# A GPS layer on one core: marks in POOL's gather queue, a rearranged first part, a look-up accumulated in PSUM, and packing operands read from PSUM

## The chip, the core and the metric

The kernel runs on one core of one Trainium2 chip. The core has a matrix engine (PE, whose weight loads the profile lists as PEld), a vector engine (DVE), an activation engine (ACT), a general engine (POOL) and a queue engine (SP), each with an instruction stream of its own that is executed in order; they meet through semaphores. The metric is the device time of one launch in microseconds (us), the median of several runs. The profile is one further execution, taken by the hardware profiler.

## What is computed

One layer over 6250 nodes of 256 features with 206,250 edges (200,000 and one self loop per node), all in fp32. The three parts, cut to what matters:

```python
xn = layernorm(x)
# 1. graph attention, 4 heads of 64 features
h = xn @ W;  el = h @ Wl.T;  er = h @ Wr.T
e = exp(leaky_relu(el[src] + er[dst], 0.2))
w = e / segment_sum(e, src)[src]
gnn = elu(stack([segment_sum(w[:, k:k+1] * h[dst], src) for k in range(4)]) + b)
# 2. linear attention, 4 heads of 32, with 4 memory keys and values
q, k, v = split(xn @ w_qkv)            # softmax of q over features, of k over nodes
mix = rmsnorm(context(softmax(k), v) . softmax(q) @ w_out) + xn
x = x + gnn + mix
# 3. mixture of 8 experts, top 2, hidden width 256
t = layernorm(x)
x = x + t + sum_e combine[:, e] * (gelu(t @ w1[e]) @ w2[e])
```

The edges come sorted by dst, and the sums run over src.

## The kernel before

The nodes are cut into 49 tiles of 128 rows (NT), the edges into 1612 columns of 128.

**First part.** `project` takes groups of four tiles. It computes the layernorm statistics, the normalised rows xn (DVE, L310), their transposes (PE, L316), and one product pr with all the projection weights (L321). From pr, ACT copies q, k and v (L325) and a row of a table, which holds the 64 features of h and its er values (L328). DVE copies el (L329) and keeps a running maximum kmax of k (L335). SP stores four tiles of the table to memory. Between the groups run the 51 calls of `sort_batch`, which sort the edges of 32 columns (BW) by source tile pair: a one-hot ob of the bin, counts n_ps per column by PE (L371), their running sum on DVE (L375) and, by subtraction, the counts before each column (L380), ranks by two matmuls (L398, L399: `tri` is a strictly upper triangular matrix), which ACT casts to r16 (L404), DVE multiplies by ob (L410) and sums over the 26 bins (L413). L415 writes each rank twice, side by side, since the 16-bit DVE operations of this kernel work on pairs. A permutation matmul then lays the edges of each bin together in `grid` (L433). Last, `context` computes exp(k − max) (L468, L469) and the context of the linear attention, interleaved with the remaining sort batches.

**Main part.** It runs over the 25 pairs of node tiles. `pack(q)` brings the edges of one pair into 36 columns per tile (CW; 35 of them, CPT, hold edges). For 101 blocks of edges, 16 at a time, DVE builds the one-hots ohc (L858) and ohp (L870) by comparing positions with an iota, and rc (L865, twice) as the product of ohc and the packed values of grid; PE multiplies them into s_ps (L875). From s_ps come the table rows to fetch, dst_x (L884, L886), and the rows within the tile, loc (L894). `gather` then issues 35 indirect DMAs per tile on POOL (L906), 1715 in all, each of which fetches 128 table rows into a column of an xe tile. An xe tile has seven columns, a node tile needs five of them, and the pool has eight. `pack(q + 1)` is called while the first tile of pair q is summed.

`look(b, k)` fetches el for each edge: a one-hot oh of loc (DVE, L919), its transposes (PE, L932, and ACT, L936), a product with three bf16 summands of el (e_ps, L939), and a reduction over the three (er, L943). The edges of a tile lie in four quarters (S) of rows; a quarter's columns begin at multiples of eight (CS) and reach 12 columns (GC), so that neighbours overlap. `weights` adds the overlapping er together (L960, L961, L963, L964), adds the gathered er part of xe (L967, five times), and applies leaky ReLU and exp; the result ew_s is written to a PSUM tile named bank (L972). `sums(k)` multiplies oh by ew_s (ohw, L980) and PE accumulates 45 products with xe into a_ps (L987). The xe tiles are free when their last product is done.

Between these steps a generator puts in the attention outputs and the expert products of earlier blocks of four tiles (h_ps L731, y_ps L747, x L751, store L759). A tile scheduler turns dependencies into semaphore waits and keeps each engine's order as it lays it out. On POOL a gather waits for loc or dst_x only where it is the first of its pack, for the freeing of an xe tile at the first of seven columns, and, always, for the landing of the gather eight back.

**Tail.** After the last tile follow the remaining expert steps and a branch for overfull tiles, which these data do not take.

Of the kernel before, what the change touches and what calls it, by code (L numbers as in the profile page):

```python
# [17 lines left out]
P = 128  # L18
GT = 4
# [6 lines left out]
EB = 7  # L26
S = 4
# [8 lines left out]
def tile_gps_layer(  # L36
# [174 lines left out]
    tri = sp.tile([P, P], F16, name="tri")  # L211
    nc.vector.tensor_scalar(tri, iota_f, piota, None, op0=OP.is_gt)
# [3 lines left out]
    starts = sp.tile([NB, BW // CB, CB], F32, name="starts")  # L216
    nc.vector.memset(starts, 1.0)
    nc.vector.memset(starts[:, :, 0:1], 0.0)
# [69 lines left out]
    def project(t0, n):  # L288
# [16 lines left out]
        tab = qw.tile([P, GT, TW], F32, name="tab")  # L305
        nc.gpsimd.memset(tab[:, :, TW - 1:TW], 1.0)  # L306
        for j in range(n):
            t = t0 + j
            xn = qw.tile([P, D], F32, name="xn")
            nc.vector.tensor_scalar(  # L310
                xn, xt[:, j, :], stats[:, t, 0:1], rstd[:, t:t + 1],
                op0=OP.subtract, op1=OP.mult,
# [15 lines left out]
            nc.scalar.copy(tab[:, j, :TW - 1], pr[:, O_TAB:O_EL])  # L328
            nc.vector.tensor_copy(el[:, t, :], pr[:, O_EL:PW])  # L329
            rows = P if t < NT - 1 else last  # L330
            k_t = kv[:rows, t, :HID]
            if t == 0:
                nc.vector.tensor_copy(kmax, k_t)
            else:
                nc.vector.tensor_max(kmax[:rows], kmax[:rows], k_t)  # L335
        nc.sync.dma_start(
            out=table[t0 * P:(t0 + n) * P, :].rearrange("(t p) f -> p t f", p=P),
            in_=tab[:, :n, :],
# [9 lines left out]
    def sort_batch(t):  # L348
# [20 lines left out]
        n_ps = sps.tile([NB, BW], F32, name="n_ps")  # L369
        for c in range(w):  # L370
            nc.tensor.matmul(  # L371
                n_ps[:, c:c + 1], lhsT=ob[:, c, :], rhs=ones16[:, 0:1], start=True, stop=True
            )
        inc = sw.tile([NB, BW], F32, name="inc")
        nc.vector.tensor_tensor_scan(  # L375
            inc[:, :w], flat(starts)[:, :w], n_ps[:, :w], 0.0,
            op0=OP.mult, op1=OP.add,
        )
        before = sw.tile([NB, BW, 2], F16, name="before")
        nc.vector.tensor_tensor(  # L380
            before[:, :w], inc[:, :w, None].to_broadcast([NB, w, 2]),
            n_ps[:, :w, None].to_broadcast([NB, w, 2]), op=OP.subtract,
        )
        if w == BW:
            nc.scalar.copy(ntot[:, bs], inc[:NQ].rearrange("q (b c) -> q b c", c=CB)[:, :, CB - 1])
        else:
            for b, e in enumerate(ends):
                nc.scalar.copy(ntot[:, bs][:, b:b + 1], inc[:NQ, e - 1:e])
        ahead = sw.tile([NB, BW, NB], F16, name="ahead", bufs=1)
        nc.vector.tensor_tensor(  # L390
            pairs(ahead[:, :w]), two(before[:, :w], NB // 2), row(delta, NB // 2), op=OP.mult
# [3 lines left out]
        for i, a in enumerate(range(0, w, BB)):  # L395
            z = min(w, a + BB)
            part = r_ps[:, i, :(z - a) * NB]
            nc.tensor.matmul(part, lhsT=tri, rhs=flat(ob[:, a:z]), start=True, stop=False)  # L398
# [12 lines left out]
        rank = sw.tile([P, BW], F16, name="rank")  # L411
        with nc.allow_low_precision("one summand of each sum is not zero"):
            nc.vector.tensor_reduce(rank[:, :w], r16[:, :w], axis=AX.X, op=OP.add)  # L413
        rank2 = sw.tile([P, BW, 2], F16, name="rank2")
        nc.vector.tensor_copy(rank2[:, :w], rank[:, :w, None].to_broadcast([P, w, 2]))  # L415
# [25 lines left out]
    def context():  # L441
        km_ps = mps.tile([HID, P], F32, name="tp")
# [23 lines left out]
        for t0, n in groups:  # L466
            kk = kv[:, t0:t0 + n, :HID]
            nc.vector.tensor_sub(kk, kk, krow[:, None, :].to_broadcast([P, n, HID]))  # L468
# [333 lines left out]
    yps = gx.enter_context(tc.tile_pool(name="yp", bufs=2, space=PSUM))  # L802

# [3 lines left out]
    gb_s = bank[:, 512 - FO:]  # L807
# [7 lines left out]
    def pack(q):  # L815
# [8 lines left out]
        for u in range(U):  # L824
# [6 lines left out]
            total = pe.tile([P, S, NBT], F32, name="e_ps")  # L831
# [21 lines left out]
        iota_2 = pairs(iota_h)[:, None]  # L853
        s_ps = pl.tile([P, 2, U * CW], F32, name="s_ps")
        for t0 in range(0, NBT, PB):
# [8 lines left out]
            for i in range(2):  # L864
                nc.vector.tensor_tensor(  # L865
                    pairs(rc[:, :m, i, :]), pairs(ohc[:, :m]),
                    twos(grid[:, q, t0:t0 + m, i, :], U * CW // 2), op=OP.mult,
# [31 lines left out]

# [15 lines left out]
    def look(b, k):  # L915
# [10 lines left out]
        elif k < 3:  # L926
# [19 lines left out]
            )  # L946

    def weights(xes, er):
        z = gw.tile([P, CW, H], F32, name="z")

        def of(q0, n, a, m):

# [225 lines left out]
```

## Time and profile before

| | us |
|---|---|
| median of 3 runs | 3158.25 |
| lowest, highest run | 3149.09, 3170.76 |
| profiled execution | 3989.86 |
| its span | 3988.1 |
| first gather begins | 491.6 |
| gathers, one | 0.944, in steps of 1.25 |
| idle of POOL ahead of gathers | 1901.0 |

The profiled execution took 831.6 us longer than the median run, so its durations are taken from it, and its span is not a measure of a run without the profiler. Its mean granted TensorE clock was 0.717 of full speed. The table by stage reads, for each stretch: its length, busy time and instructions of PE, PEld, DVE, ACT and POOL, the granted clock, the share of DMA and GB/s.

```profile
0.00:50.00 50.00, 28.16 (x247) 15.34 (x248) 39.44 (x106) 14.52 (x45) 10.28 (x28) 0.95 0.31 93
50.00:400.00 350.00, 264.87 (x3115) 158.84 (x3114) 307.00 (x699) 117.47 (x373) 1.08 (x10) 0.72 0.11 22
492.00:3852.00 3360.00, 1877.03 (x10817) 1429.43 (x10818) 1564.19 (x3578) 482.16 (x807) 1648.22 (x1709) 0.71 0.13 27
3852.00:3989.00 137.00, 113.83 (x529) 80.28 (x528) 52.86 (x168) 45.75 (x83) 6.25 (x7) 0.87 0.08 9
```

A row of a groups view gives line, engine, operation, the tiles written and read, and the count; then the busy time, the mean of one in ns, and the idle time just before them with what ended it. "remote" and "another core or an unknown queue" are the profile's names for a release whose source it did not find. A row of the waits view gives the waiting line, what released it, the time in all, the number of waits and the longest.

### The profile page before, as it was taken

How to read it: one execution, taken by the hardware profiler on the slowest of the kernel's cores; microseconds unless marked ns; L12 is line 12 of the kernel's file. 1: busy time of each engine (PE TensorE's matmuls, PEld its weight loads, DVE VectorE, ACT ScalarE, POOL GpSimd, SP SyncE). 2: the span in 40 equal slices, each digit the busy share in tenths (PEclk: the TensorE clock that was granted, in tenths of full speed). 3: DMA queues.
4: the chain of work that ended last, by engine and by line, in shares of the span. 5: the costliest groups of instructions: out<-in, count | busy, mean ns of one | idle time of the engine just before them, and what ended most of it. 6: DMA issues, size and time to landing. Idle time of an engine off the chain costs nothing.

```text
span 3988.1 us, 40348 instructions
## 1 busy us (share of the span) xinstructions
PE 2343.3 (59%) x15298; PEld 1728.2 (43%) x15298; DVE 2045.5 (51%) x4719; ACT 681.1 (17%) x1365; POOL 1666.2 (42%) x1753
## 2 busy tenths in 40 slices
PE   6787633354546666656766573573674654655758
PEld 3444423333334544444544352452453443443546
DVE  8888843456445445534625543553453445255353
ACT  3333201111111211211211110110110101101113
POOL 1000076544654454463454545436345444545430
PEclk8776556666667877776868686686786776776879
DMA  1001012111211111110111101101011011111110
GB/s 57 28 21 17 13 26 45 29 38 43 46 47 48 27 19 23 21 35 14 26 19 23 25 17 26 22 14 33 16 21 28 18 23 21 21 21 25 19 20 9
DMA packets 106684, 103.98 MB, mean 26 GB/s; under 512 B 42726, under 2 KB 78788, under 8 KB 106484
## 3 DMA queue, kind: packets, MB, share of 16 engines
q0 software_dynamic: 54880, 60.70, 9.0%
q1 hardware_dynamic: 49908, 39.75, 3.5%
q8 instruction: 122, 2.00, 0.2%
q10 hardware_dynamic: 1696, 0.89, 0.1%
q14 instruction: 78, 0.64, 0.1%
HBM read 86.57 MB, written 14.65 MB: 25 GB/s over the span
## 4 chain that ended last, share of the span: by engine, by line
another core or an unknown queue 30%; PE 26%; DVE 19%; issue 5%; ACT 3%; POOL 1%; DMA 0%; DVEq 0%; ACTq 0%; POOLq 0%
PE y_ps L747 7%; PE a_ps L987 7%; PE h_ps L731 7%; DVE rc L865 4%; DVE ohp L870 4%; DVE ohc L858 2%; DVE ohw L980 2%; PE s_ps L875 1%; PE y_ps L722 1%; POOL xe L906 1%; PE y_ps L671 1%; PE t_ps L932 1%; PE y_ps L559 1%; ACT ohT L936 1%
## 5 line engine op out<-in xcount | busy, mean ns | idle before, releaser
L906 POOL DMA_INDIRECT xe<-table,dst_x x1715 | 1654.9, 965 | 1901.0 <-issue 767.3
L987 PE MATMUL a_ps<-ohw,xe 128*65 128x128 f32 x4410 | 693.8, 316 | 295.5 <-issue 171.5
L987 PEld LDWEIGHTS a_ps<-ohw,xe 128*65 128x65 f32 x4410 | 614.6, 165 | 392.3 <-issue 229.9
L980 DVE TENSOR_TENSOR ohw<-oh,bank 128x1280 f32<-128x1280 bf16 x196 | 322.6, 1649 | 631.6 <-remote 524.3
L731 PE MATMUL h_ps<-tokT,w1s 128*128 128x512 f32 (+2 forms) x896 | 438.9, 609 | 176.0 <-ACT hT L739 173.3
L747 PE MATMUL y_ps<-w2s,hT 128*128 128x256 f32 x1568 | 434.9, 420 | 73.6 <-DVE x L751 44.1
L747 PEld LDWEIGHTS y_ps<-w2s,hT 128*128 128x128 f32 x1568 | 323.5, 213 | 196.2 <-issue 94.1
L751 DVE SCALAR_TENSOR_TENSOR x<-y_ps,comb,x 128x256 f32<-128x256 f32 x392 | 186.6, 481 | 379.8 <-PE y_ps L747 198.3
L875 PE MATMUL s_ps<-rc,ohp 128*128 128x144 f16 x2525 | 241.3, 264 | 164.9 <-DVE rc L865 156.4
L875 PEld LDWEIGHTS <-ohp 128*128 128x128 f16 x2525 | 219.2, 116 | 216.8 <-issue 127.5
L731 PEld LDWEIGHTS h_ps<-tokT,w1s 128*128 128x128 f32 x896 | 166.3, 210 | 291.8 <-ACT hT L739 198.5
L739 ACT ACTIVATE hT<-h_ps,b1s 128x512 f32<-128x512 f32 (+2 forms) x224 | 142.0, 634 | 828.3 <-PE h_ps L731 379.7
L865 DVE TENSOR_TENSOR rc<-ohc,grid 128x1152 f16<-128x1152 f16 (+1 forms) x350 | 229.1, 693 | 5.2 <-remote 5.2
L870 DVE TENSOR_TENSOR ohp<-to,iota_h 128x2048 f16<-128x2048 f16 (+1 forms) x175 | 195.1, 1115 | 24.6 <-remote 16.4
L722 PE MATMUL y_ps<-b2s,cTs 8*128 8x256 f32 x98 | 53.3, 640 | 208.9 <-issue 107.9
L936 ACT COPY ohT<-t_ps 128x768 bf16<-128x768 bf16 x98 | 78.1, 797 | 334.1 <-remote 144.7
L939 PE MATMUL e_ps<-elw,ohT 128*128 128x48 bf16 x588 | 39.9, 199 | 157.5 <-ACT ohT L936 84.5
L858 DVE TENSOR_TENSOR ohc<-to,iota_h 128x1152 f16<-128x1152 f16 (+1 forms) x175 | 121.3, 694 | 8.8 <-ACT to L851 8.8
L722 PEld LDWEIGHTS y_ps<-b2s,cTs 8*128 8x128 f32 x98 | 21.9, 276 | 230.2 <-issue 122.6
L932 PE MATMUL t_ps<-identb,oh 128*128 128x128 bf16 x588 | 68.6, 269 | 86.7 <-DVE oh L919 79.0
L306 POOL MEMSET tab<- 128x4 f32 x13 | 1.3, 108 | 282.0 <-DMA table<-tab 282.0
L723 DVE TENSOR_TENSOR x<-x,y_ps 128x256 f32<-128x256 f32 x49 | 20.5, 421 | 191.6 <-remote 83.9
(261 smaller groups left out, 2748.6 us busy)
## 6 DMA issues: line engine op xcount, KB each, us to landing
xe<-table,dst_x POOLq DMA_INDIRECT x1715
xt<-in_x_dram SPq DMA_DIRECT2D x24, 512.0 KB
base_y<-xt SPq DMA_DIRECT2D x12, 512.0 KB
yt<-base_y SPq DMA_DIRECT2D x11, 512.0 KB
out_dram<-x SPq DMA_DIRECT2D x11, 512.0 KB
w1s<-in_L_ffn_w_dram SPq DMA_DIRECT2D x8, 256.0 KB
w2s<-in_L_ffn_w_dram SPq DMA_DIRECT2D x8, 256.0 KB
table<-tab SPq DMA_DIRECT2D x12, 138.0 KB
```

Source lines behind the costliest of these rows:

```text
L731: nc.tensor.matmul(h_ps[:, :w], lhsT=w1s[:, e, c, f * P:(f + 1) * P], rhs=held["tokT"][:, c, :w], start=(c == 0), stop=(c == DC - 1),)
L739: nc.scalar.activation(held[e][:, f, :w], h_ps[:, :w], AF.Gelu, bias=b1s[:, k:k + 1])
L747: nc.tensor.matmul(y_ps, lhsT=held[e][:, f, j * P:(j + 1) * P], rhs=w2s[:, e, f, :], start=(f == 0), stop=(f == FC - 1),)
L751: nc.vector.scalar_tensor_tensor(x2[:, j, :], y_ps, held["comb"][:, j, e:e + 1], x2[:, j, :], op0=OP.mult, op1=OP.add,)
L858: nc.vector.tensor_tensor(pairs(ohc[:, :m]), twos(to[:, 0, t0:t0 + m], U * CW // 2), iota_2[:, :, :U * CW // 2].to_broadcast([P, m, U * CW ...
L865: nc.vector.tensor_tensor(pairs(rc[:, :m, i, :]), pairs(ohc[:, :m]), twos(grid[:, q, t0:t0 + m, i, :], U * CW // 2), op=OP.mult,)
L870: nc.vector.tensor_tensor(pairs(ohp[:, :m]), twos(to[:, 1, t0:t0 + m], P // 2), iota_2.to_broadcast([P, m, P // 2, 2]), op=OP.is_equal,)
L875: nc.tensor.matmul(flat(s_ps), lhsT=ohp[:, t - t0, :], rhs=flat(rc[:, t - t0]), start=(t == 0), stop=(t == NBT - 1),)
L906: nc.gpsimd.indirect_dma_start(out=xe[:, j, :], out_offset=None, in_=table, in_offset=bass.IndirectOffsetOnAxis(ap=dst_x[:, c:c + 1], axis=0),
L936: nc.scalar.copy(ohT, t_ps)
L980: nc.vector.tensor_tensor(ohw[:, :n], oh[:, g0:g1, i, None, :].to_broadcast([P, n, H, SN]), ew_s[:, c0:c0 + n, :, None].to_broadcast([P, n ...
L987: nc.tensor.matmul(a_ps[:, i].rearrange("f h n -> f (h n)"), lhsT=xes[c // EB][:, c % EB, H:], rhs=ohw[:, c - c0].rearrange("p h n -> p (h ...
```

## The change

The changed kernel differs in four places.

**Marks.** Each call of the indirect DMA goes through `in_turn`. Ahead of each group of four gathers (MG) POOL gets a no-op; dependencies without a semaphore keep the order no-op, gather, gather, gather, gather, and the fourth gather waits for the no-op by a semaphore. The wait for the landing of an earlier gather then moves into a separate semaphore instruction.

**First part.** xn is computed by ACT, as scale times x plus a shift that DVE computes for each group. el is no longer copied from PSUM tile by tile by DVE: the table row is wider and takes el too, POOL copies el from it for each group, and only then writes the constant column. The running maximum becomes one reduction over all tiles in `context`. In the sort, each count stands beside a zero, so that the running sum comes out in pairs at once; the ranks are inclusive (`upto` in place of `tri`), and the subtraction goes. The ranks are added half to half before the reduction, and ACT writes the pairs. POOL does the subtraction of the maximum from k.

**Look-up.** e_ps is one PSUM tile for all 36 columns of a node tile. A matmul of one zero row clears it, and the twelve products of the four quarters accumulate into their overlapping columns. One reduction over the three summands gives z. The tile `total` of a pack moves to the PSUM pool of t_ps.

**Packing operands.** The iota that ohc and ohp compare with, the iota of oh, and the values of grid for the pair at hand, copied in each pack, lie in bank as 16-bit values.

```diff
-    tri = sp.tile([P, P], F16, name="tri")
-    nc.vector.tensor_scalar(tri, iota_f, piota, None, op0=OP.is_gt)
-    starts = sp.tile([NB, BW // CB, CB], F32, name="starts")
+    starts = sp.tile([NB, BW // CB, CB, 2], F32, name="starts")
...
+    one_none = sp.tile([P, 2], F16, name="one_none")
+    nc.vector.memset(one_none, 0.0)
+    nc.vector.memset(one_none[:, 0:1], 1.0)
...
+        shift = qw.tile([P, GT], F32, name="shift")
+        nc.vector.scalar_tensor_tensor(
+            shift[:, :n], stats[:, t0:t0 + n, 0], -1.0, rs, op0=OP.mult, op1=OP.mult
+        )
+        tab = qw.tile([P, GT, TW - 1 + H], F32, name="tab")
...
-            nc.vector.tensor_scalar(
-                xn, xt[:, j, :], stats[:, t, 0:1], rstd[:, t:t + 1],
-                op0=OP.subtract, op1=OP.mult,
+            nc.scalar.activation(
+                xn, xt[:, j, :], AF.Identity, bias=shift[:, j:j + 1], scale=rstd[:, t:t + 1]
             )
...
-            nc.scalar.copy(tab[:, j, :TW - 1], pr[:, O_TAB:O_EL])
-            nc.vector.tensor_copy(el[:, t, :], pr[:, O_EL:PW])
-            rows = P if t < NT - 1 else last
-            k_t = kv[:rows, t, :HID]
-            if t == 0:
-                nc.vector.tensor_copy(kmax, k_t)
-            else:
-                nc.vector.tensor_max(kmax[:rows], kmax[:rows], k_t)
+            nc.scalar.copy(tab[:, j, :], pr[:, O_TAB:PW])
+        nc.gpsimd.tensor_copy(el[:, t0:t0 + n, :], tab[:, :n, TW - 1:])
+        nc.gpsimd.memset(tab[:, :n, TW - 1:TW], 1.0)
...
-                n_ps[:, c:c + 1], lhsT=ob[:, c, :], rhs=ones16[:, 0:1], start=True, stop=True
+                n_ps[:, c, :], lhsT=ob[:, c, :], rhs=one_none, start=True, stop=True
...
-        before = sw.tile([NB, BW, 2], F16, name="before")
-        nc.vector.tensor_tensor(
-            before[:, :w], inc[:, :w, None].to_broadcast([NB, w, 2]),
-            n_ps[:, :w, None].to_broadcast([NB, w, 2]), op=OP.subtract,
+            flat(inc[:, :w]), starts.rearrange("q b c two -> q (b c two)")[:, :2 * w],
+            flat(n_ps[:, :w]), 0.0, op0=OP.mult, op1=OP.add,
         )
...
-            nc.tensor.matmul(part, lhsT=tri, rhs=flat(ob[:, a:z]), start=True, stop=False)
+            nc.tensor.matmul(part, lhsT=upto, rhs=flat(ob[:, a:z]), start=True, stop=False)
...
+        fold = NB // 4 * 2
+        nc.vector.tensor_tensor(
+            r16[:, :w, :fold], r16[:, :w, :fold], r16[:, :w, NB - fold:], op=OP.add
+        )
         with nc.allow_low_precision("one summand of each sum is not zero"):
-            nc.vector.tensor_reduce(rank[:, :w], r16[:, :w], axis=AX.X, op=OP.add)
+            nc.vector.tensor_reduce(
+                rank[:, :w], r16[:, :w, :NB - fold], axis=AX.X, op=OP.add
+            )
-        nc.vector.tensor_copy(rank2[:, :w], rank[:, :w, None].to_broadcast([P, w, 2]))
+        nc.scalar.copy(rank2[:, :w], rank[:, :w, None].to_broadcast([P, w, 2]))
...
+        nc.vector.tensor_reduce(
+            kmax, kv[:, :NT - 1, :HID].rearrange("p t d -> p d t"), axis=AX.X, op=OP.max
+        )
+        nc.vector.tensor_max(kmax[:last], kmax[:last], kv[:last, NT - 1, :HID])
...
-            nc.vector.tensor_sub(kk, kk, krow[:, None, :].to_broadcast([P, n, HID]))
+            nc.gpsimd.tensor_sub(kk, kk, krow[:, None, :].to_broadcast([P, n, HID]))
...
+    none = gw.tile([1, (1 + CPT) * 3 * H], BF16, name="none", bufs=1)
+    nc.vector.memset(none, 0.0)
-    gb_s = bank[:, 512 - FO:]
+    gb_s = bank[:, CPT * H:CPT * H + FO]
...
+    edges = bank[:, words:words + 2 * NBT]
+    nc.vector.tensor_copy(iota_p, iota_h.bitcast(F32))
+    nc.vector.tensor_copy(iota_q, iota_b[:, :SN].bitcast(F32))
+    iota_p, iota_q = iota_p.bitcast(F16), iota_q.bitcast(BF16)
...
-            total = pe.tile([P, S, NBT], F32, name="e_ps")
+            total = pt.tile([P, S, NBT], F32, name="t_ps")
...
-        iota_2 = pairs(iota_h)[:, None]
+        nc.vector.tensor_copy(
+            edges, grid[:, q].rearrange("p t i two -> p (t i two)").bitcast(F32)
+        )
+        edges_q = edges.bitcast(F16).rearrange("p (t i two) -> p t i two", i=2, two=2)
+        iota_2 = pairs(iota_p)[:, None]
...
-                    twos(grid[:, q, t0:t0 + m, i, :], U * CW // 2), op=OP.mult,
+                    twos(edges_q[:, t0:t0 + m, i, :], U * CW // 2), op=OP.mult,
...
+    def in_turn(issue):
+        i = len(issued)
+        if i % MG == 0:
+            marks.append(nc.gpsimd.nop())
+            if i:
+                behind(marks[-1], issued[-1], mybir.DependencyClass.NoSync)
+        row = issue()
+        if i % MG == 0:
+            behind(row, marks[-1], mybir.DependencyClass.NoSync)
+        else:
+            behind(row, issued[-1], mybir.DependencyClass.NoSync)
+        if i % MG == MG - 1:
+            behind(row, marks[-1], mybir.DependencyClass.Sync)
+        issued.append(row)
...
-                nc.gpsimd.indirect_dma_start(
+                in_turn(lambda: nc.gpsimd.indirect_dma_start(
...
-                pairs(iota_b[:, :SN])[:, None].to_broadcast([P, GC * S, SN // 2, 2]),
+                pairs(iota_q)[:, None].to_broadcast([P, GC * S, SN // 2, 2]),
...
-            e_ps = pe.tile([P, gh, S, 3, H], F32, name="e_ps")
+            if k == 1:
+                nc.tensor.matmul(
+                    e_ps.rearrange("p c i h -> p (c i h)"), lhsT=identb[0:1, :], rhs=none,
+                    start=True, stop=False,
+                )
             for g in range(gh):
                 nc.tensor.matmul(
-                    e_ps[:, g].rearrange("p s i h -> p (s i h)"), lhsT=ohT[:, g, :],
-                    rhs=elw[:, b].rearrange("p s i h -> p (s i h)"), start=True, stop=True,
-                )
-            nc.vector.tensor_reduce(
-                er[:, g0:g0 + gh].rearrange("p g s h -> p (g s) h"),
-                e_ps.rearrange("p g s i h -> p (g s) h i"), axis=AX.X, op=OP.add,
-            )
+                    e_ps[:, g0 + g::CS][:, :S].rearrange("p s i h -> p s (i h)"),
+                    lhsT=ohT[:, g, :],
+                    rhs=elw[:, b].rearrange("p s i h -> p s (i h)"),
+                    start=False, stop=(g0 + g == GC - 1),
+                )
...
-        nc.vector.tensor_copy(of(0, S, 0, CS), er_of(0, S, 1, CS))
-        nc.vector.tensor_copy(z[:, CPT - more:CPT], er[:, GC - more:, S - 1])
-        head, tail = of(1, S - 1, 0, more), of(0, S - 1, CS - 1, 1)
-        nc.vector.tensor_add(head, head, er_of(0, S - 1, GC - more, more))
-        nc.vector.tensor_add(tail, tail, er_of(1, S - 1, 0, 1))
+        nc.vector.tensor_reduce(
+            z, e_ps[:, 1:].rearrange("p c i h -> p c h i"), axis=AX.X, op=OP.add
+        )
```

In the instruction order of the changed kernel DVE's results of the experts (x, L751) lie between the steps of a pack, the additions of xe (z, L967) of a pair's second tile lie inside the pack, and two of the four products ohw of the pair's first tile (L980) move from ahead of the pack to behind it. DVE has 1213 semaphore instructions where it had 974, POOL 1113 where it had 300; ACT has 144 table loads where it had 138.

## The prediction

> **What bounds the kernel now.** I read the page's busy rows, its chain, the waits of POOL and DVE, a table by stage, and one timeline.
>
> ```profile
> span 3988.1 us, 40348 instructions
> PE 2343.3 (59%) x15298; PEld 1728.2 (43%) x15298; DVE 2045.5 (51%) x4719; ACT 681.1 (17%) x1365; POOL 1666.2 (42%) x1753
> another core or an unknown queue 30%; PE 26%; DVE 19%; issue 5%; ACT 3%; POOL 1%; DMA 0%; DVEq 0%; ACTq 0%; POOLq 0%
> L906 POOL DMA_INDIRECT xe<-table,dst_x x1715 | 1654.9, 965 | 1901.0 <-issue 767.3
> ```
>
> The reader is to see that no engine is busy for 60% of the span, and that the chain's largest entry, 30% or 1200 us, names no engine of this core. What it is, the DVE waits and a table by stage inside one run of gathers show (columns: us; busy PE, PEld, DVE, ACT, POOL; granted clock; DMA share; GB/s):
>
> ```profile
> DVE ohw L980 <- remote: 524.3, 35, 29.7
> 2408.00:2415.00 7.00, 2.69 (x27) 1.78 (x25) 6.31 (x24) 1.12 (x2) 4.74 (x6) 0.93 0.34 95
> 2422.00:2429.00 7.00, 1.23 (x5) 0.73 (x5) 0.00 (x0) 0.00 (x0) 5.17 (x7) 0.66 0.12 25
> 2436.00:2443.00 7.00, 0.00 (x0) 0.00 (x0) 0.00 (x0) 0.00 (x0) 5.28 (x6) 0.50 0.14 29
> 2443.50:2448.50 5.00, 2.77 (x13) 2.77 (x14) 1.77 (x2) 0.00 (x0) 0.00 (x0) 0.50 0.03 7
> ```
>
> POOL begins gathers at 2408.7. Some ten microseconds later PE slows, then PE, DVE and ACT have no row at all, and within a microsecond of POOL's stopping (2443.4) they run again:
>
> ```profile
> 2442.44 0.94 POOL L906 DMA_INDIRECT xe<-table,dst_x  x1 [0.30 <-issue]
> 2443.92 1.75 DVE L980 TENSOR_TENSOR ohw<-oh,bank 128x1536 f32<-128x1536 bf16 x1 [26.59 <-remote]
> 2448.55 0.94 POOL L906 DMA_INDIRECT xe<-table,dst_x  x1 [5.17 <-PE a_ps L987]
> ```
>
> Counted from the rows between 492 and 3852 us, PE, DVE and ACT are all empty for 993 us, 840 of them while POOL gathers. The profiled execution took 3989.9 us, the median run 3158.3: a surplus of 831.6, nearly the same number. So at least most of the burst stall belongs to that execution. [...] By the chain, 3990 − 1200 = 2790, the median still holds 368 us of it. No row here separates the two; I keep both ends.
>
> The undisturbed bound is then POOL with its waits. A gather steps 1.25 us (0.944 and a gap of 0.30). First gather 491.6 (its 187.4 us wait for loc, L894) + 1715 × 1.25 = 2144 + 128 from the last gather to the end = 2764. The median lies 394 above: POOL waiting for index packs (26 to 28 us a pair of tiles, on 25 pairs) and for xe buffers.
>
> ```profile
> POOL xe L906 <- PE a_ps L987: 350.6, 55, 23.5
> POOL xe L906 <- DVE loc L894: 187.4, 1, 187.4
> 400.00:492.00 92.00, 59.44 (x598) 44.33 (x595) 82.05 (x173) 21.16 (x57) 0.41 (x1) 0.59 0.02 5
> ```
>
> **The change, part by part.**
>
> *First part, 0 to 491.6 us.* DVE is busy for 87% of it (the first three stages: 428 of 492 us), and POOL can begin only when it is over, so DVE time taken out here comes off the end.
>
> ```profile
> L310 DVE TENSOR_SCALAR xn<-xt,stats,rstd 128x256 f32<-128x256 f32 x49 | 19.7, 406 | 16.1 <-PE tp L316 15.5
> L335 DVE TENSOR_TENSOR kmax<-kmax,kv 128x128 f32<-128x128 f32 x47 | 13.3, 282 | 2.7 <-ACT kv L325 2.6
> L413 DVE TENSOR_REDUCE rank<-r 128x32 f16<-128x832 f16 x50 | 50.1, 1003 | 0.0
> L380 DVE TENSOR_TENSOR before<-inc,n_ps 26x64 f16<-26x64 f32 x50 | 9.9, 198 | 0.0
> L415 DVE COPY rank<-rank 128x64 f16<-128x64 f16 x50 | 9.0, 180 | 0.0
> L468 DVE TENSOR_TENSOR kv<-kv,krow 128x512 f32<-128x512 f32 x12 | 8.0, 670 | 0.0
> ```
>
> Consecutive DVE rows overlap by some 0.08 us, so 49 rows are worth about 4 us less than their sum. xn goes to ACT: −16, +2 for 13 shifts. kmax: −10, +7 for one strided reduce of 6144 elements (1.2 ns each, L413's rate). The el copy (49 × 160 ns) goes to POOL: −4. before: −6. rank2 to ACT: −5. The fold: L413 (832 elements, 1.00 us) becomes a half-size f16 add (0.32 by L410's rate) and a reduce of 416 to 448 elements (0.54): −6 over 50. The scan is twice as long: +2. kv sub to POOL: −8. tri: −3. Sum −47. ACT (a third busy) takes on 49 × 0.42 + 50 × 0.2 = 30 us; rank2 there puts a DVE, ACT, DVE round trip into each batch, up to 0.5 × 50 = 25 us if no other batch fills it. On POOL the copies, memsets and 13 subs wait ahead of no gather, and POOL is busy for 12 us in this part; behind them wait only SP's table and eltab stores, which the first gather needs and which come with the DVE end in any case. Bounds −60 to −20; taken −45.
>
> *Look-up added in PSUM.* Per tile DVE loses two L943 reduces (0.45 each), L960, L961, L963, L964 (0.23, 0.16, 0.19, 0.16) and gains one reduce of 420 elements (0.65): −0.6 net of overlap. This lies between the last gather and the weights, whose successors (L980, L987) free the xe buffers that POOL waits for: −30 over 49. PE gains a zero matmul of one row and 432 columns (0.49 by L832's 404): +24 us, beside other work; its 59% covers it, and without cover it costs those 24. It puts e_ps accumulation in one bank in order, with er's reader one step later. DVE also gets about 240 more semaphore waits (each z add waits on its own gathers) at 50 ns: +12, and 25 copies of edges (0.35): +9. Six more ACT table loads (1.28 each): +8, off the path. Net on the path −30 to +10; taken −15.
>
> *Packing operands in PSUM.* L858, L865 ×2, L870 (ohc, rc, ohp) and L919 (oh) read one of two 16-bit operands from PSUM.
>
> ```profile
> L865 DVE TENSOR_TENSOR rc<-ohc,grid 128x1152 f16<-128x1152 f16 x300 | 214.2, 752 | 5.2 <-remote 5.2
> L870 DVE TENSOR_TENSOR ohp<-to,iota_h 128x2048 f16<-128x2048 f16 x150 | 182.9, 1220 | 24.6 <-remote 16.4 <-PE s_ps L875 4.4 <-ACT to L851 3.8
> L980 DVE TENSOR_TENSOR ohw<-oh,bank 128x1536 f32<-128x1536 bf16 x98 | 171.7, 1752 | 614.9 <-remote 524.3 <-PE a_ps L987 38.8 <-issue 33.7
> ```
>
> rc takes 0.65 ns an element; L980, which reads f32 from PSUM and writes f32, takes 1.14. Those are the two ends. [...] By it the five rows go to 1.05 ns an element (the slope between L980's 1280 and 1536) plus 0.13: 1152 elements to 1.35 us, 2048 to 2.28; a pack (seven groups of up to 16 blocks) grows by some 18 us, 24 packs by 440 us on POOL's path. [...] By that the rows stay, and what is left to gain is the 36 us by which 85 of the 1715 gathers exceed 0.944[...]. The trace has no 16-bit PSUM read by DVE, but L838, 404 f32 with one PSUM operand, takes 0.568 and L841, SBUF alone, 0.574[...]. I take 2×, a gain of 0 to 36, taken −10, and keep 1× as the slower rival.
>
> *Marks.* Each fourth gather now waits for a semaphore that a no-op ahead of its group sets, and its own wait for the gather eight back moves to a separate instruction: 429 marks, POOL's semaphore instructions from 300 to 1113. What stands behind each wait on POOL is the other gathers, then everything that reads xe. It can cost one more gap per group, 429 × 0.30 = +129, or, with a restart of 1.9 us per group as after buffer waits, +815. It can gain if it cuts POOL's run-ahead (in the timeline its sequencer stands some six gathers ahead of the gather being made)[...]: between 0 and all of the 368 to 394 us above. POOL, without packs and buffers, idles about 8 us per tile, so part of a gap is covered. I take −80: a fifth of the upper gain, since the mark stops POOL for less than a microsecond in five, against the 5 us pause after which the engines ran on.
>
> Sum: −45 − 15 − 10 − 80 = −150, 3158 → about 3000 us. This is for unprofiled runs; against the profiled execution's own 3989.9 the first three parts give −70, and the marks anything up to −840 where that stall ends. I use the median for the forecast.
>
> **Rivals.** *Marks open the whole stall* (2715 to 2930, about 2820): 3158 − 70 − 270. For: 368 left by the chain. Against: the surplus 832 ≈ 840 leaves nothing of it. *First part only* (3080 to 3127): the marks neither gain nor cost. *No change* (3127 to 3190): marks cost what the first part gives; half of 129 plus ACT's round trips. *Slower, PSUM at single rate* (3190 to 3600): 3158 − 45 − 15 + 440 = 3538 and no gain from marks. It decides at the mean of the rc row: below 0.8 us the forecast stands, above 1.0 packs are the bound and it is slower. The marks' gap at 0.30 to 1.9 us, uncovered, also ends here.
>
> **How the numbers follow.** Forecast (2930 to 3080) 0.45; whole stall 0.24; first part only 0.08; no change 0.06; slower 0.17. About 1%, 32 us, is what a measurement of this kernel can tell from no change. Faster: 0.77, same 0.06, slower 0.17. The range from 2760 to 3200 leaves out most of the slower case (0.15) and the lowest fifth of the stall's (0.05).
>
> **What would show it.** Right: the first gather at about 445 us; rc at 0.75 us for 1152 elements; steps of 1.25 us within a group and no more than 1.6 across a mark; DVE rows during gathers, the chain's unknown share well below 30%. Wrong: rc near 1.35 us; gaps over 1 us at each fourth gather; the first gather still at 480, with rank2 on ACT ending DVE's waits; or a profiled time far below the old one while the median stays, which would say that the stall was the profiler's alone.

## The result, and the profile after

The changed kernel takes 3382.6 us (median of 4 runs, 3379.7 to 3385.8) against 3156.7 us: a ratio of 1.071 with a 95% interval of 1.067 to 1.075. It is slower by 226 us. The profiled execution took 3385.8 us, so here the profile describes the median run.

From the page of the changed kernel, its busy row and two groups (busy in us and mean of one in ns, then the idle time ahead with what ended most of it). Line numbers have moved: L906 is now L957, L967 is L1009, L865 is L891, L987 is L1028. (Each kernel of the experiments has line numbers of its own.)

```profile
PE 2198.9 (65%) x15347; PEld 1617.6 (48%) x15347; DVE 1988.0 (59%) x4307; ACT 721.7 (21%) x1471; POOL 1691.1 (50%) x1779
...
L957 POOL DMA_INDIRECT xe<-table,dst_x x1715 | 1642.8, 958 | 1253.6 <-PE a_ps L1028 630.1
...
L1009 DVE TENSOR_TENSOR z<-z,xe 128x28 f32<-128x28 f32 x245 | 44.8, 191 | 753.2 <-DMA xe<-table,dst_x 741.8
```

The reader is to see two things. No engine is busier than 65%. And DVE waits 742 us at one small operation, the addition of xe to z, for gathers to land. It waited there before as well: a kernel of the experiments, b_marks, which differs from the kernel before by the marks alone and takes the same time, has 531 us of it. What matters is what stands behind the wait.

The timeline of one pair of the changed kernel shows it (start, duration, engine, line, operation, count, idle before and its releaser):

```profile
2378.22 0.19 DVE L1009 TENSOR_TENSOR z<-z,xe 128x28 f32<-128x28 f32 x1 [7.06 <-DMA xe<-table,dst_x]
...
2384.41 0.94 POOL L957 DMA_INDIRECT xe<-table,dst_x  x1 [0.30 <-issue]
...
2387.62 0.19 DVE L1009 TENSOR_TENSOR z<-z,xe 128x28 f32<-128x28 f32 x1 [8.99 <-DMA xe<-table,dst_x]
...
2388.42 0.75 DVE L884 TENSOR_TENSOR ohc<-to,bank 128x1152 f16<-128x1152 f16 x1
...
2415.33 0.23 DVE L910 SCALAR_TENSOR_TENSOR dst_x<-s_i,hi 128x72 int32<-128x72 int32 x1
...
2416.59 0.94 POOL L957 DMA_INDIRECT xe<-table,dst_x  x1 [31.24 <-PE a_ps L1028]
```

These additions belong to the second tile of the pair. They stand in DVE's queue ahead of the first ohc of the next pack, and the last of them waits for the last gather of the pair, begun at 2384.41. Only then does the pack begin (2388.42); it takes 27 us to dst_x (2415.33), and POOL, which has no more rows to fetch, starts again 1 us later after 31 us of idleness. The profile names a_ps as the releaser, since a product of it had just ended; but in all 24 packs of this kernel POOL's first gather begins 0.74 to 0.77 us after the end of the pack's second dst_x, so what came last is dst_x.

The same place in the kernel before is seen in the timeline of b_marks:

```profile
2236.45 0.75 DVE L859 TENSOR_TENSOR ohc<-to,iota_h 128x1152 f16<-128x1152 f16 x1
...
2259.43 1.03 POOL L932 DMA_INDIRECT xe<-table,dst_x  x1 [0.30 <-issue]
...
2262.14 0.22 DVE L885 SCALAR_TENSOR_TENSOR dst_x<-s_i,hi 128x72 int32<-128x72 int32 x1
...
2263.34 0.18 DVE L993 TENSOR_TENSOR z<-z,xe 128x28 f32<-128x28 f32 x1
...
2263.41 0.94 POOL L932 DMA_INDIRECT xe<-table,dst_x  x1 [2.96 <-issue]
```

There the pack runs while POOL still gathers, dst_x is ready 2 us after the last gather, and the additions come behind it. Not every pair is so: the late pairs alternate in b_marks between about 2 us and about 19 us of idleness of POOL, and in the changed kernel between 31 and 22.

The whole difference can be added up from POOL's rows, since POOL gathers from its first gather to the last. "Gathers" are the 1715 rows with the gaps of at most 1 us between them; "idle" are the longer gaps.

| us | first gather | gathers | idle | last gather to end | span |
|---|---|---|---|---|---|
| b_marks (like before) | 495.3 | 2254 | 273 | 128 | 3151.0 |
| after | 459.9 | 2158 | 638 | 127 | 3383.9 |
| difference | −35 | −96 | +365 | −1 | +233 |

Two terms brought a gain, 131 us together. It was lost almost three times over in waits of POOL; of the 638 us, 624 lie ahead of the first gather of a pair.

### The profile page after: what moved, and what is told of

It reads as the page before. It is cut to its first block, busy times and chain, and to the rows that moved or that the text cites. A ratio compares the mean times of both kernels' runs of the same rounds, so it can differ in the third digit from the quotient of the medians.

```text
span 3383.9 us, 41196 instructions
## 1 busy us (share of the span) xinstructions
PE 2198.9 (65%) x15347; PEld 1617.6 (48%) x15347; DVE 1988.0 (59%) x4307; ACT 721.7 (21%) x1471; POOL 1691.1 (50%) x1779
## 5 line engine op out<-in xcount | busy, mean ns | idle before, releaser
L957 POOL DMA_INDIRECT xe<-table,dst_x x1715 | 1642.8, 958 | 1253.6 <-PE a_ps L1028 630.1
L1028 PE MATMUL a_ps<-ohw,xe 128*65 128x128 f32 x4410 | 599.0, 295 | 241.7 <-issue 179.3
L1028 PEld LDWEIGHTS a_ps<-ohw,xe 128*65 128x65 f32 x4410 | 552.6, 152 | 277.3 <-issue 194.1
L1009 DVE TENSOR_TENSOR z<-z,xe 128x28 f32<-128x28 f32 x245 | 44.8, 191 | 753.2 <-DMA xe<-table,dst_x 741.8
L757 PE MATMUL y_ps<-w2s,hT 128*128 128x256 f32 x1568 | 402.0, 393 | 108.7 <-DVE x L761 90.9
L891 DVE TENSOR_TENSOR rc<-ohc,bank 128x1152 f16<-128x1152 f16 (+1 forms) x350 | 227.6, 693 | 1.1
L896 DVE TENSOR_TENSOR ohp<-to,bank 128x2048 f16<-128x2048 f16 (+1 forms) x175 | 195.0, 1114 | 0.0
L987 ACT COPY ohT<-t_ps 128x768 bf16<-128x768 bf16 x98 | 78.2, 798 | 275.5 <-PE t_ps L983 275.3
L884 DVE TENSOR_TENSOR ohc<-to,bank 128x1152 f16<-128x1152 f16 (+1 forms) x175 | 121.3, 693 | 0.0
L428 DVE TENSOR_TENSOR ohp<-rank,iota_h 128x4096 f16<-128x4096 f16 (+1 forms) x51 | 115.7, 2269 | 2.9 <-ACT rank L421 2.9
L326 PE MATMUL pr<-wcat,xT 128*128 128x456 f32 x196 | 109.5, 688 | 4.9 <-ACT xT L323 4.0
L434 PE MATMUL g_ps<-rv,ohp 128*128 128x52 f16 x1612 | 65.8, 204 | 40.0 <-DVE ohp L428 40.0
```

Of the source, the lines that this page charges most:

```text
L428: nc.vector.tensor_tensor(pairs(ohp[:, :w]), two(rank2[:, :w], P // 2), row(iota_h, P // 2), op=OP.is_equal)
L757: nc.tensor.matmul(y_ps, lhsT=held[e][:, f, j * P:(j + 1) * P], rhs=w2s[:, e, f, :], start=(f == 0), stop=(f == FC - 1),)
L884: nc.vector.tensor_tensor(pairs(ohc[:, :m]), twos(to[:, 0, t0:t0 + m], U * CW // 2), iota_2[:, :, :U * CW // 2].to_broadcast([P, m, U * CW ...
L891: nc.vector.tensor_tensor(pairs(rc[:, :m, i, :]), pairs(ohc[:, :m]), twos(edges_q[:, t0:t0 + m, i, :], U * CW // 2), op=OP.mult,)
L896: nc.vector.tensor_tensor(pairs(ohp[:, :m]), twos(to[:, 1, t0:t0 + m], P // 2), iota_2.to_broadcast([P, m, P // 2, 2]), op=OP.is_equal,)
L957: in_turn(lambda: nc.gpsimd.indirect_dma_start(out=xe[:, j, :], out_offset=None, in_=table, in_offset=bass.IndirectOffsetOnAxis(ap=dst_x[: ...
```

## The experiments

First an order theory (the loss comes from the changed order of DVE's instructions) was tried against two rivals, that the marks or the look-up cost the time. Brackets give 95% intervals of the ratio to the kernel before; of the diffs the main lines are shown.

**b_marks**: the kernel before with `in_turn` around its gathers, nothing else.

> The kernel before with the marks alone. Order theory (the loss is the changed order of DVE, in which the products ohw of the quarters 2 and 3 and with them the end of a tile stand behind the next pack, and additions of xe stand ahead of or inside it; that order comes with the packing operands in PSUM): DVE's order is untouched here, so 3158 us within 1%, with the profiled execution falling from 3990 to about the same figure. Marks theory (POOL's waits for its marks cost the time): about 3380 us, and gaps above 0.30 us at every fourth gather.

Measured 3152.4 us, ratio 0.9997 (0.9983 to 1.0012). The marks neither gain nor cost: the gap between two gathers is 305 ns by the median at each of the four places of a group.

**b_psum**: the kernel before with the packing operands in PSUM.

```diff
+    iota_p, iota_q = iota_p.bitcast(F16), iota_q.bitcast(BF16)
...
-                    twos(grid[:, q, t0:t0 + m, i, :], U * CW // 2), op=OP.mult,
+                    twos(edges_q[:, t0:t0 + m, i, :], U * CW // 2), op=OP.mult,
```

> The kernel before with the packing operands in PSUM alone. Order theory: DVE has the order of the changed kernel, so 3370 to 3450 us (the loss of 226 us without the gain of the first part), rc at 0.752 us as before. Marks theory: 3158 us within 1%. Look-up theory (the loss is the accumulated look-up): 3158 us within 1%.

Measured 3421.7 us, 1.0853 (1.0817 to 1.0888). This part alone brings more than the whole loss.

**a_nopsum**: the changed kernel without that part (the same lines, turned round).

> The changed kernel with the packing operands back in SBUF; first part, look-up and marks stay. Order theory: 3158 less about 31 us of the first part and up to 30 of the look-up, so 3090 to 3130 us. Marks theory and look-up theory: about 3380 us.

Measured 3343.2 us, 1.0611 (1.0575 to 1.0648): a miss. The loss is in the kernel with the PSUM operands alone and in the kernel without them.

**b_order**: the kernel before, with the products of quarters 2 and 3 put behind the pack, as in the changed kernel.

```diff
+        if i == 2 and "rc" in newest:
+            tc.add_manual_dep(
+                row.ins, newest["rc"].ins.name,
...
```

> The kernel before with one more edge of order on DVE and nothing else: ohw of quarter 2 of a pair's first tile comes behind the last rc of the pack. Order theory: 3350 to 3450 us. Marks, look-up, or the PSUM operands themselves as the cause: 3158 us within 1%.

Measured 3167.5 us, 1.0054 (1.0021 to 1.0087): a miss. In 23 of 24 packs the products stand as in the changed kernel, two ahead and two behind, and that costs half a per cent. What is left of the order theory is its other half, the additions. The order in which DVE's instructions stand can be counted in each kernel: all five additions of the second tile stand ahead of the first rc in 0 of 24 packs in the kernel before and in b_marks, in 2 in b_order, in 7 in a_nopsum, in 12 in b_psum and in the changed kernel. So the kernel has the bad order with the PSUM operands alone and, less often, without them; b_look below shows that the look-up alone brings it too. That is why taking out one part did not help. Why the scheduler lays out the additions so for either part was not looked into.

**b_wait** puts that one wait into the kernel before:

```diff
     def pack(q):
+        if q and q * U - 1 in ready:
+            held = nc.vector.tensor_copy(seen_x, ready[q * U - 1][0][-1][:, EB - 1, :H])
...
+            if held and t0 == 0:
+                tc.add_manual_dep(
+                    row.ins, held.ins.name,
...
```

> The kernel before with one copy of 4 columns on DVE, ahead of the first ohc of each pack, that reads the last gather of the pair's second tile; it makes DVE wait for that gather and does nothing else. Theory of the additions: each of the 24 packs begins only when the pair's gathers have landed, POOL idles about 31 us in place of 11 on the mean, so 3155 + 24 x 20 = 3600 to 3660 us. Rival: a wait of DVE ahead of the pack is hidden, 3155 us within 1%.

Measured 3598.6 us, 1.1425 (1.1406 to 1.1445). Its waits of DVE (in all, times, longest, us):

```profile
DVE seen_x L819 <- DMA xe<-table,dst_x: 440.2, 24, 28.9
```

One copy of four columns costs 449 us (3598.6 against 3149.7), just under the range expected. Mean idle of POOL ahead of a pair is 33.3 us, where b_marks has 10.9. The mechanism is shown by itself. That 449 is close to the 440 us that DVE waits is chance: by POOL's rows the idle time grew by 532 us, and the gathers took 85 us less, of which 39 instead of 223 run beside the rows of a pack or oh.

**a_zlater** takes it out of the changed kernel:

```diff
+        with tc.issue_after(newest["rc"].ins):
+            for k, xe in enumerate(xes):
+                zk = z[:, k * EB:(k + 1) * EB]
+                nc.vector.tensor_add(zk, zk, xe[:, :, :H])
```

> The changed kernel with one edge of order more: the five additions of xe to z of each tile come behind the last rc of the newest pack on DVE. All else stays. In the changed kernel all five additions of a pair's second tile stand ahead of the pack in 12 of 24 packs, and DVE waits there for that tile's gathers. Theory of the additions: those 12 packs begin some 20 us earlier, POOL's 31 us idle after them goes to about 2, the other packs stay, so 3383 - 12 x 29 = about 3035 us, below the kernel before. Rival (the accumulated look-up, the PSUM operands or the marks cost time of their own): 3300 us or more.

Measured 3162.0 us, 1.0043 (1.0029 to 1.0057). The sign is right: one edge of order brings back 221 of the 226 us (3382.6 − 3162.0, in two groups of runs, with the kernel before at 3156.7 and 3149.7). The size is a miss: idle of POOL is 418 us, 220 less than in the changed kernel and still 145 more than in b_marks, which uses up the gains of the first part and the gathers. The trace says why. Counted over the late pairs, which alternate, from the end of the first tile's last gather on POOL, the pack begins at 31.7 us in the repaired pairs, where b_marks has 24.2; dst_x comes 26.1 instead of 25 us after that; and the pair's gathers end at 44.8 instead of 48.7. So POOL's idle there fell from 31.5 to 14.2 us and not to 2. The first comes with the experts' routing (tok, lg), which here stands ahead of the pack and waits for PE; what lengthens the second was not separated. The third is the gain of the gathers itself: where the next thing to come is dst_x, a pair whose gathers end 4 us sooner waits 4 us longer.

**b_look**: the kernel before with the look-up alone.

```diff
-            seen[b] = oh, gw.tile([P, GC, S, H], F32, name="er")
+            seen[b] = oh, pe.tile([P, 1 + CPT, 3, H], F32, name="e_ps")
...
```

> The kernel before with the look-up accumulated in PSUM alone. In its order all five additions stand ahead of the pack in 7 of 24 packs. Theory of the additions: 3155 + 7 x 29 less some 10 to 30 us for the lighter path = 3330 to 3360 us. Rival (the look-up as forecast, shorter by its DVE work): 3125 to 3155 us.

Measured 3374.4 us, 1.0717 (1.0699 to 1.0735). More than expected: beside the 7 packs behind their additions, in the late part the other packs begin at 52 to 54 us instead of 41, behind 24 results of the experts (x, L751) where b_marks has 16, and DVE waits for PE at them. a_nopsum has the same starts and the same count. So in these two kernels the additions are not the whole cause; no run here moves the x alone. By POOL's rows: gathers −9 us, idle +236 against b_marks. The lighter path to the weights is not seen in it.

**a_zlater_prio**: as a_zlater, with the packs at a higher priority in the scheduler.

> As a_zlater, and the instructions of a pack are given a higher priority in the scheduler, so that they come ahead of the experts' results x on DVE, behind which the other half of the packs begins. If the late start of those packs (38 us after the first tile's gathers) comes from x ahead of them: POOL's idle of 22 us on 12 packs falls too, so 3035 - 100 to - 250 = 2790 to 2930 us. If the pack's own matmuls on PE stand behind the experts' products there: 3035 us within 1%.

Measured 3106.1 us, 0.9856 (0.9838 to 0.9874): 1.4% faster than the kernel before, but outside both ranges. It moved the repaired pairs (pack at 22 us, idle 11.7) but not the others (37.6 and 21.4).

The next four move the pack a whole tile forward, into the time in which DVE waits for gathers, with the additions behind it:

```diff
-                if k == 1 and b % U == 0 and b + U < NT:
-                    pack(b // U + 1)
+                if k == 1 and b % U == U - 1 and b + 1 + U < NT:
+                    pack((b + 1) // U + 1)
```

**a_early**, the changed kernel so:

> The changed kernel with each pack called one tile earlier (in the second tile of the pair before last, so that DVE builds it while it would wait for the next pair's first gathers), and the additions of xe kept behind the newest pack. All parts of the change stay. If what is lost is POOL's wait for the next pack, that wait goes to about nothing: first gather 455 + 1715 x 1.26 + 128 from the last gather to the end = 2744, so 2740 to 2830 us, faster than both kernels. If another engine binds next (DVE 59% busy, PE 65%), 2900 us or more.

Measured 3118.0 us, 0.9895 (0.9866 to 0.9925), far above the 2740 to 2830 hoped for. The wait ahead of a pair is gone (0.4 us on the mean), and another took its place: 357 us at the first gather of the pair's second tile, 23 times. By POOL's waits it is for the freeing of xe:

```profile
POOL xe L957 <- PE a_ps L1029: 369.7, 54, 32.6
```

**a_early_nopsum**:

> As a_early, with the packing operands back in SBUF. With POOL as the bound the mean gather shows in the end time: it takes 1.01 us where DVE reads both operands from SBUF and 0.96 with one in PSUM, so 1715 x 0.054 = 93 us more than a_early. If the operands' place does not matter by itself: the same as a_early within 1%.

Measured 3057.1 us, 0.9699 (0.9674 to 0.9725), the other way round than expected. Its gathers take 2302 us against 2168, 134 us more, but POOL idles 184 us instead of 361. In the tile in which the pack is called, two of the four products ohw stand behind the pack in a_early; here three or four stand ahead of it, in 22 of 23 packs. That fits, but is not shown as the cause.

**a_early_nomarks**:

> As a_early, without the marks. Marks inert: the same as a_early within 1%. If the marks let other engines on during long runs of gathers: slower than a_early by 1% or more, since the runs are longest here; if they cost a wait: faster.

Measured 3117.9 us against 3118.0. The marks are inert in this order too.

**b_early**, no part of the change:

> The kernel before with the same two edits (pack one tile earlier, additions behind it) and no part of the change: 492 + 1715 x 1.31 + 128 = 2870 to 2950 us. Beside a_early it gives what the change is worth where order does not decide: about 35 us of the first part and 93 of the gathers, 128 in all.

Measured 3024.4 us, 0.9593 (0.9568 to 0.9618), above the range expected. This is the fastest kernel of the study, and it holds none of the four parts: two edits of order are worth 127 us on the kernel before. It does not give the worth of the change beside a_early, as was hoped, since the scheduler puts all four products ahead of the pack here in 22 of 23 packs and two in a_early.

The last six runs fell on a chip on which the kernel before itself took 3960 and 3952 us. Five of them were to show whether the products behind the pack hold the xe tiles, by putting all four ahead of it:

```diff
+                if k == S - 1 and b % U == U - 1 and b + 1 + U < NT:
+                    with tc.issue_after(newest["w"].ins):
+                        pack((b + 1) // U + 1)
```

**a_early_sums**, **b_early_sums** and, with the pack at its old place, **a_sums**:

> As a_early, but a pack comes behind all four products ohw of the tile in which it is called, so that the products free the xe tiles before the pack begins. In a_early POOL idled 357 us at one place, 23 times: the first gather of a pair's second tile, which waits for the xe tiles that the late products of the tile before hold. If the products behind the pack are that wait, the 357 us go: 3118 - 357 = 2760, so 2740 to 2850 us. If it is another wait: 3050 us or more.

> The kernel before with the same order and no part of the change: no wait at pairs, gathers of 1.02 to 1.06 us: 495 + 1715 x 1.34 + 128 = 2920, so 2880 to 3020 us. The difference to a_early_sums is the worth of the change where the order of DVE is the same in both: 40 us of the first part and some 100 to 150 of the gathers.

> The changed kernel with the pack at its old place, the additions of xe behind it and all four products ohw of the tile ahead of it, so that DVE's order in this respect is that of the kernel before in every pair. If the loss of the changed kernel is the order alone, it is faster than the kernel before by the first part and the gathers as far as POOL's waits allow: 3030 to 3120 us. If part of the loss lies elsewhere: 3150 us or more.

Measured 4020.3 us (1.0151, 1.0107 to 1.0196), 4006.3 us (1.0118, 1.0071 to 1.0165) and 4157.8 us (1.0497, 1.0454 to 1.0540). Run again as **a_sums2** and **a_early_sums2**, they fell on the same chip:

> The kernel of a_sums once more: the changed kernel with the pack at its old place, the additions of xe behind it and all four products ohw of the tile ahead of it. Its first run fell on a chip on which the kernel before took 3960 us, and is no test. On a chip where the kernel before takes 3155 us: 3030 to 3120 us if the loss is the order alone, 3150 us or more if part of it lies elsewhere.

> The kernel of a_early_sums once more, for the same reason: the pack one tile earlier, behind all four products ohw of that tile, ahead of the additions. On a chip where the kernel before takes 3155 us: 2740 to 2850 us if the late products were what held the xe tiles in a_early (3118 us); 3050 us or more if it was another wait.

Measured 4184.6 us (1.0568, 1.0526 to 1.0609) and 4075.5 us (1.0330, 1.0272 to 1.0387). All five are slower there than the kernel before. On that chip none answers the question, which stays open.

**b_first**, the first part alone, ran on that chip too:

> The kernel before with the lighter first part alone; DVE's order in the main part is as before. The first gather comes some 35 us earlier and nothing else changes: 3105 to 3125 us. If the earlier start is given back in the main part: 3155 us within 1%.

Measured 3929.4 us beside 3960.3 on that chip, 0.9917 (0.9862 to 0.9973): 31 us less by the medians, with the first gather at 457.5 us. The part keeps its gain there; the times that were expected hold for another chip.

## Why the prediction was wrong

**The bound.** The prediction took POOL with its waits as the bound and subtracted each gain from the end. The experiments show a loop instead: gathers of a pair's first tile, then DVE's work up to dst_x, then the next pair. A change counts by what it does to that loop. Its DVE part, from the end of the first tile's last gather on POOL to dst_x, is 56.7 us on the mean in b_marks, 69.7 in the changed kernel, 60.5 in a_zlater. The sum of the prediction had no term for it.

**The step that failed** is in the look-up paragraph: "DVE also gets about 240 more semaphore waits (each z add waits on its own gathers) at 50 ns: +12". It priced the instruction that waits and not the wait: 50 ns is the median of the 608 semaphore instructions that DVE has at these additions in the trace before, and the longest of them took 6.9 us. DVE waits there in any order (b_marks; in all, times, longest, us):

```profile
DVE z L993 <- DMA xe<-table,dst_x: 531.0, 65, 28.4
```

The changed kernel has 742 us, a_zlater, where the additions stand behind the pack, 532. In place of +12 there are 211 us more of waiting on DVE; what stands behind it in the bad packs is the next pack, who waits for the pack is POOL, and POOL has 365 us more idle time. The document's own description of the change, ahead of the prediction, says that these additions lie inside the pack; counting in how many packs all five stand ahead of it (12 of 24) would have given 12 × 26 us, the time from the first ohc of a pack to dst_x in the first trace, or some 310 us, as an estimate before any run. The "net on the path −30 to +10" of the same paragraph was for b_look 225 us the other way (3374.4 against 3149.7), in part by the additions. The paragraph on the packing operands lacks the same term: forecast at −10, b_psum measured 267 us more (3421.7 against 3154.9).

**The marks**, taken at −80 us, were worth nothing (0.9997; 3117.9 and 3118.0). That term had no row behind it: it is a fifth of 368 to 394 us, and the 368 come from mixing two executions, the chain's unknown 1200 us of the one of 3990 us and the median of 3158.

The reading of the surplus of the first profile over the median was wrong as well. The prediction set the surplus of 831.6 us beside 840 us in which POOL gathers and PE, DVE and ACT have no row, and gave most of that stall to the execution. But the profiled execution of b_marks took 3152.8 us, its median 3152.4, while the kernel before took 3945 to 3980 us in all 14 of its runs on one of the chips. Counted between the first and the last gather (weight loads with PE, gaps between gathers up to 1 us as gathering), b_first has there 975 us without a row of PE, DVE and ACT, 811 of them while POOL gathers, and the first profile has 987 and 821. So the stall goes with that chip, or its condition then, and not with the profiler. And not all of it is stall: b_marks, on a chip without it, still has 446 us of such time, all while POOL gathers, so that 832 and 840 nearly agree was chance. The stall also stood with the marks: a_early_sums has 1001 and 818. The kernel before with only the marks was not tried on that chip, nor was the changed kernel.

**The operands in PSUM** were right in rate and too small in gain. The prediction set two rates side by side, that of rc in the profile before (0.65 ns an element, the prediction's 2×) and that of L980, which reads f32 from PSUM (1.14, its 1×), and the row was to decide which holds with a 16-bit operand in PSUM. It did: the form of 1152 elements takes 0.752 us in the profile before and, with one operand in PSUM, here:

```profile
L891 DVE TENSOR_TENSOR rc<-ohc,bank 128x1152 f16<-128x1152 f16 x300 | 212.8, 752 | 0.8
```

So rc with its 16-bit operand in PSUM keeps its rate here, 0.752 us in both, and the reason of the slower rival is out: its 1.35 us for the row was an estimate at the slope of L980. The gain was put at 0 to 36 us from the excess of 85 gathers over 0.944; that the place of DVE's operands made them long was the author's estimate, with no row behind it. The figure came from a trace in which only 56 gathers lay for more than half of their time under the rows concerned (ohc, rc, ohp, oh); in b_marks 223 do. In b_marks the gathers take 1014 ns on the mean, in b_psum 960:

```profile
L932 POOL DMA_INDIRECT xe<-table,dst_x x1715 | 1738.9, 1014 | 980.1 <-issue 424.8 <-DVE loc L895 191.3 <-PE y_ps L748 173.3
```

```profile
L920 POOL DMA_INDIRECT xe<-table,dst_x x1715 | 1645.8, 960 | 1346.2 <-PE a_ps L1001 569.7 <-issue 467.8 <-DVE loc L908 190.5
```

That is 1715 × 0.054 = 93 us. Part of such a gain can come from packs that no longer run beside gathers: b_wait, without an operand in PSUM, has 39 gathers under such rows and a mean of 964. What the operands do by themselves is seen in a_early and a_early_nopsum, below. The pair of lines also shows how the gain was lost: idle ahead of the gathers went from 980 to 1346.

**The first part** was right in kind, −35 for −45. Rows of the changed kernel in the first 460 us name two terms that were mis-sized:

```profile
L417 DVE TENSOR_REDUCE rank<-r 128x32 f16<-128x448 f16 x50 | 29.9, 598 | 0.0
L413 DVE TENSOR_TENSOR r<-r 128x384 f16<-128x384 f16 x50 | 17.8, 356 | 0.0
L448 DVE TENSOR_REDUCE kmax<-kv 128x128 f32<-128x6144 f32 x1 | 11.0, 11044 | 0.0
```

The fold and the shorter reduction take 598 + 356 = 954 ns where the reduction alone took 1003: −2.5 us over 50, not −6. The strided maximum costs 11 us, 1.8 ns an element and not 1.2. The first gather came at 460 us where 445 was forecast.

**Among the rivals** none had the right mechanism. The slower rival had the right sign and a right place, "packs are the bound", but the pack was late by where it stood in a queue and not by its own rate; that 3382.6 us lies in its range (3190 to 3600) is luck.

## What to carry to other kernels

Where an engine executes in order, as DVE does here (in b_wait one waiting copy of four columns held up what stands behind it, at a cost of 449 us), price a moved instruction by what stands behind it: count, in the instruction order itself, how often a wait for a late transfer stands ahead of the work that starts the next transfers. An edit that touches no order can still change it where a scheduler decides, so compare the orders of the two kernels for the few instructions that close the loop, and pin them with an edge where it matters. A faster engine gains nothing while the loop that feeds it is longer than its work (in the changed kernel POOL gathers for 96 us less than in b_marks and idles for 365 us more); look for that loop before subtracting anything.

## What the runs showed of the hardware

In these runs a gather on POOL took longer beside certain rows of DVE. In b_marks the 223 gathers that lie for more than half of their time under ohc, rc, ohp or oh, whose two 16-bit operands both come from SBUF, take 1.293 us on the mean; the 1417 without such rows take 0.965. In b_early, where packs lie under gathers more often, 286 take 1.484. With one operand in PSUM, in the changed kernel, it is 0.951 for 122 of them and 0.958 for the rest. The cleanest pair is a_early and a_early_nopsum, in both of which packs run beside gathers: 264 gathers under such rows take 0.946 us with an operand in PSUM, 321 take 1.354 without. In b_marks, a gather beside rc and one after the pack's end:

```profile
2257.62 1.50 POOL L932 DMA_INDIRECT xe<-table,dst_x  x1 [0.30 <-issue]
2258.22 1.42 DVE L866 TENSOR_TENSOR rc<-ohc,grid 128x1152 f16<-128x1152 f16 x2
...
2264.66 0.95 POOL L932 DMA_INDIRECT xe<-table,dst_x  x1 [0.31 <-issue]
```

The same program takes 3150 to 3155 us on three of the four chips met in the experiments and 3952 to 3960 us on the fourth. There PE, DVE and ACT are without a row together for 975 us between the first and the last gather (b_first), where b_marks on another chip has 446. What was faster elsewhere need not be so there: a_early and b_early gained 1% and 4% on another chip, and with the products ahead of the pack as well, which was tried on the fourth alone, their kernels lost 1.5 to 3.3% and 1.2% (a_early_sums, b_early_sums). Whether the edge or the chip did that, and what differs between the chips, stays open.
